# First sums of a graph network: overflow heads loaded alone, gathers two blocks ahead

## The chip, the cores and the metric

One core of a Trainium2 chip runs the whole program in one launch. The metric is the device time in microseconds of that core. The profile is of one execution of the program.

## The reference

The program is a stack of four graph layers over the same graph of 6250 nodes and 200000 edges, each with a residual and a layer norm before it. Two of the layers sum, over the edges of a node, a gated value of the node at the other end. Cut to what the change touches, the first layer computes:

```
gate = silu(edge_attr @ F1W + F1b) @ F2W + F2b
ei = emb[atom_z[src]];  ej = emb[atom_z[dst]]
gate = gate + (ei * (ej @ adapt)).sum(-1, keepdims=True)
msg = gate * h[dst] * (cw * mj)[:, None]
agg = segment_sum(msg, src, N)
tot = clip(segment_sum(mj, src, N), 1e-08)
```

The third layer has the same shape with other weights. Both logits, of the first and third layer, come out of the same pass over the edges (`G` = 32 values of `ei` for each).

## The kernel before

The nodes are padded to 49 blocks (`NB`) of 128 nodes (`P`). An earlier stage sorts the edges into a grid in DRAM: for each node of a block one slot for each of the 49 blocks that an edge can lead to. Each slot is a record of 138 floats (`RW`, 552 bytes), whose column 137 (`HD`) is the head, the number of the node at the other end, or zero where the slot is empty. Edges that find their slot taken go to overflow slots: block `b` has `WS[b]` of them per node, between 4 and 28, 502 over all blocks.

The function `first_sums` runs over the blocks in the order of the list `ORDER`. For one block the 49 slots per node go in four pieces of 14 columns (`PC`; the last one has 7). For these grid pieces the partner's values are picked without a gather: the heads are broadcast (`hr`), compared with the lane number on DVE (`hot_b`, L1187), converted on ACT (L1191) and stored; PE multiplies the one-hot matrices with the table that sits in SBUF (L1007) and ACT copies the result out as `tr` (L1008). The tile `tr` has two buffers. PE also transposes the one-hot matrices (L1198) and ACT gathers them into the tile `dt` (L1199), one row of an adjacency matrix for each node.

The overflow slots are in no block in particular. So their partner's values come by indirect DMA, issued by POOL, one for each slot column (L1085, `tr_o`), from the table in DRAM; the index is worked out on DVE from the head column. One more indirect DMA for each block brings the block's own values `ei` (L1073). The inner function `add` (L1152 to L1178) treats one piece of records, of the grid or of the overflow: bias, product with `ei`, gate, sums on DVE, and copies on ACT that are stored to DRAM. For overflow pieces the addition of the bias is kept in its place in the program by `keep_in_program_order`.

At the end of a block `put_rows` stores the 128 rows of the adjacency matrix (`adj`, one indirect DMA on POOL, L1231). The overflow edges are then written into these rows as single bytes, again by indirect DMAs on POOL, one for each slot column (`put_cells`, L1112). They must wait until the row store has landed. Their addresses (`to`) and values (`many`) are worked out in `overflow` (L1087 to L1107).

What sets the order: each engine executes its instructions in the order of the built program, which a scheduler derives from the source, from the tiles' buffers and from dependencies. Loads of records, of `hr` and the store of the heads are issued by SP. Record tiles (`recs`) form a ring of 8 buffers, shared by grid and overflow pieces; `tr_o` has one buffer of 28 columns, `ei` two. The source's order at the end of a block is:

```
i = put_rows(tc, g.adj, g.nat, b, dt..., "adj")
...
    others, ei, own_cells = overflow(after, hd)
put_cells(*cells_of)
```

In the built program POOL's order in a block is: row store, byte stores of the same block, `ei` of the next block, gathers of the next block.

Of the kernel before, what the change touches and what calls it, by code (L numbers as in the profile page):

```python
# [18 lines left out]
F32 = mybir.dt.float32  # L19
# [5 lines left out]
OP = mybir.AluOpType  # L25
# [4 lines left out]
N, E, H, R, G, NEL, L = 6250, 200000, 48, 40, 32, 119, 4  # L30
P = 128
BIG = 1.0e30
# [3 lines left out]
def rows(t, i):  # L36
    return bass.IndirectOffsetOnAxis(ap=t[:, i : i + 1], axis=0)
# [436 lines left out]
NB = 49  # L474
NQ = NB * P
# [54 lines left out]
def chunks(n, k):  # L530
    return [(i, min(k, n - i)) for i in range(0, n, k)]
# [480 lines left out]
def first_sums(ctx: ExitStack, tc: tile.TileContext, g, keep, dram, table0, tails, h, agg, tot):  # L1012
# [39 lines left out]
    def load(b, spans, src):  # L1052

        out = []
        for s0, n in spans:
            t = sp.tile([P, PC, RW], F32, name="recs", bufs=8)
            if src is over:
                nc.sync.dma_start(t[:, :n], over[b, :, s0 : s0 + n])
            else:
                for k in range(s0, s0 + n, GD):  # L1060
                    v = g.grid[k * NQ : (k + GD) * NQ].rearrange("(r d) f -> r d f", d=GD)
                    nc.sync.dma_start(t[:, k - s0 : k - s0 + GD], v[b * P : (b + 1) * P])
            out.append(t)
        return out

    def overflow(b, hd):


        W = WS[b]
        spans = chunks(W, PC)  # L1070
        recs = load(b, spans, over)
        ei = sp.tile([P, 2 * G + H], F32, name="ei")
        nc.gpsimd.indirect_dma_start(out=ei, out_offset=None, in_=tails, in_offset=rows(g.nat, b))  # L1073
        hv = hd[:, NB : NB + W]
        for (s0, n), t in zip(spans, recs):
            nc.vector.tensor_copy(hv[:, s0 : s0 + n], t[:, :n, HD])
        none = sp.tile([P, OS], F32, name="none", bufs=1)
        nc.vector.tensor_scalar(none[:, :W], hv, 0.0, None, OP.is_equal)
        nc.vector.tensor_scalar(g.bias[:, g.col[b] + NB : g.col[b] + NB + W], none[:, :W], -BIG, None, OP.mult)
        ix = g.idx[:, WO[b] : WO[b + 1]]  # L1080
        nc.vector.tensor_scalar(none[:, :W], none[:, :W], float(NQ), -1.0, OP.mult, OP.add)
        nc.vector.tensor_tensor(ix, hv, none[:, :W], OP.add)
        tr = sp.tile([P, OS, T0], F32, name="tr_o", bufs=1)
        for w in range(W):
            nc.gpsimd.indirect_dma_start(out=tr[:, w], out_offset=None, in_=table0, in_offset=rows(g.idx, WO[b] + w))  # L1085

        mf = sp.tile([P, OS], F32, name="times", bufs=1)  # L1087
        for w, n in chunks(W, 12):
            eq = sp.tile([P, 12, NB + OS], BF, name="same", bufs=1)
            nc.vector.tensor_tensor(eq[:, :n, : NB + W], hd[:, None, : NB + W].to_broadcast([P, n, NB + W]),  # L1090
                                    hv[:, w : w + n, None].to_broadcast([P, n, NB + W]), OP.is_equal)
            nc.vector.tensor_tensor(eq[:, :n, NB : NB + W], eq[:, :n, NB : NB + W],
                                    weights[:, w : w + n, :W], OP.mult)
            nc.vector.reduce_sum(mf[:, w : w + n], eq[:, :n, : NB + W], AX.X)

        to = sp.tile([P, OS], I32, name="to")
        nc.vector.scalar_tensor_tensor(none[:, :W], mf[:, :W], float(AGAIN), none[:, :W], OP.is_ge, OP.add)
        nc.vector.tensor_scalar(none[:, :W], none[:, :W], -1.0, float(1 << 19), OP.not_equal, OP.mult)
        nc.vector.tensor_tensor(none[:, :W], none[:, :W], nat49[:, b : b + 1].to_broadcast([P, W]), OP.add)
        pl = sp.tile([P, OS], I32, name="pl", bufs=1)  # L1100
        nc.vector.tensor_scalar(pl[:, :W], ix, 7, None, OP.logical_shift_right)
        nc.vector.tensor_tensor(to[:, :W], pl[:, :W], none[:, :W], OP.add)
        nc.vector.tensor_scalar(to[:, :W], to[:, :W], 7, None, OP.logical_shift_left)
        nc.vector.tensor_scalar(pl[:, :W], ix, P - 1, None, OP.bitwise_and)
        nc.vector.tensor_tensor(to[:, :W], to[:, :W], pl[:, :W], OP.bitwise_or)
        many = sp.tile([P, OS // 4], I32, name="times_8")
        nc.scalar.activation(many.bitcast(F8)[:, :W], mf[:, :W], AF.Copy, saturate=False)  # L1107
        return [(NB + s0, n, rec, tr[:, s0 : s0 + n]) for (s0, n), rec in zip(spans, recs)], ei, (to, many)

    def put_cells(b, to, many):  # L1110
        for w in range(WS[b]):
# [9 lines left out]
        nc.sync.dma_start(hr[:, : n * P], heads[b : b + 1, d0 * P : (d0 + n) * P].to_broadcast([P, n * P]))  # L1121
        return hr

    def heads_to_rows(b, recs):

        hd = sp.tile([P, NB + OS], F32, name="hd")
        for (s0, n), t in zip(spans, recs):
            nc.vector.tensor_copy(hd[:, s0 : s0 + n], t[:, :n, HD])
        pt = tp.tile([NB, P], F32, name="hd_ps")
        nc.tensor.transpose(pt, hd[:, :NB], ident)  # L1130
        ht = sp.tile([NB, P], BF, name="ht")
        nc.vector.tensor_scalar(ht, pt, firsts, None, OP.subtract)
        nc.sync.dma_start(heads[b].rearrange("(d p) -> d p", p=P), ht)
        bs = g.bias[:, g.col[b] : g.col[b] + NB]
        nc.vector.tensor_scalar(bs, hd[:, :NB], 1.0, -1.0, OP.min, OP.add)
        nc.vector.tensor_scalar(bs, bs, BIG, None, OP.mult)
        return [heads_of(b, *span) for span in spans[:2]], hd

    recs = load(ORDER[0], spans, g.grid)
    hrs, hd = heads_to_rows(ORDER[0], recs)  # L1140
    others, ei, own_cells = overflow(ORDER[0], hd)
    for pos, b in enumerate(ORDER):
        after = ORDER[pos + 1] if pos + 1 < NB else None
        T = NB + WS[b]
        nc.scalar.copy(h[:, pos], ei[:, 2 * G :])
        lgt = sp.tile([P, NB + OS], F32, name="lgt")
        bs = g.bias[:, g.col[b] : g.col[b] + T]
# [4 lines left out]
        def add(t0, n, rec, tr):  # L1152
            rec = rec[:, :n]
            at = sp.tile([P, PC, R], F32, name="at", bufs=2)
            nc.scalar.copy(at[:, :n], rec[:, :, :R])
            nc.scalar.dma_start(g.attr[b, :, t0 : t0 + n], at[:, :n])
            g2 = sp.tile([P, PC, H], F32, name="g2", bufs=2)
            nc.scalar.copy(g2[:, :n], rec[:, :, R + H : CW])
            nc.scalar.dma_start(g.gate[b, :, t0 : t0 + n], g2[:, :n])
            i = nc.vector.tensor_add(bs[:, t0 : t0 + n], bs[:, t0 : t0 + n], tr[:, :n, T0 - 1])  # L1160
            if t0 >= NB:
                tc.keep_in_program_order(i)

            pr = sp.tile([P, PC, 2 * G], F32, name="pr", bufs=1)
            nc.vector.tensor_mul(pr[:, :n], tr[:, :n, H : H + 2 * G], ei[:, None, : 2 * G].to_broadcast([P, n, 2 * G]))
            lg = sp.tile([P, PC, 2], F32, name="lg")
            nc.vector.reduce_sum(lg[:, :n], pr[:, :n].rearrange("p t (k g) -> p t k g", k=2), AX.X)
            nc.vector.tensor_mul(lg[:, :n, 0], lg[:, :n, 0], rec[:, :, CW])
            nc.vector.tensor_mul(lgt[:, t0 : t0 + n], lg[:, :n, 1], rec[:, :, CW])

            ga = pr[:, :, :H]
            nc.vector.tensor_add(ga[:, :n], rec[:, :, R : R + H], lg[:, :n, 0:1].to_broadcast([P, n, H]))
            if not done:
                nc.vector.memset(acc, 0.0)
            nc.vector.tensor_mul(ga[:, :n], ga[:, :n], tr[:, :n, :H])
            nc.vector.tensor_add(acc[:, :n], acc[:, :n], ga[:, :n])
            nc.vector.reduce_sum(ac[:, len(done)], tr[:, :n, T0 - 2], AX.X)
            done.append(t0)  # L1178


        dt = sp.tile([P, NB, P], F8, name="dt", bufs=1)
# [11 lines left out]
        for i, (s0, n) in enumerate(spans):  # L1193
# [6 lines left out]
            tr = sp.tile([P, PC, T0], F32, name="tr")  # L1200
            pick_rows(nc, pp, lambda d: hot[d // HC][:, d % HC * P : (d % HC + 1) * P], parts, T0, tr, s0, n, 4)
            add(s0, n, recs[i], tr)
            if i == 1 and after is not None:
                ahead = load(after, spans, g.grid)
        if after is not None:
            hrs, hd = heads_to_rows(after, ahead)
        for piece in others:
            add(*piece)
        i = put_rows(tc, g.adj, g.nat, b, dt.rearrange("p d q -> p (d q)").bitcast(I32), "adj")
        tc.declare_no_dep(i.ins, group="cells", reason="the cells before are in rows of other nodes")  # L1210
        cells_of = b, *own_cells
        nc.scalar.dma_start(g.logit[b, :, :T], lgt[:, :T])
        add_up(nc, acc, PC, agg[:, pos])
        nc.vector.reduce_sum(tot[:, pos : pos + 1], ac[:, : len(done)].rearrange("p i o -> p o i"), AX.X)
        if after is not None:
            recs = ahead
            others, ei, own_cells = overflow(after, hd)
        put_cells(*cells_of)


def add_up(nc, t, n, to):
# [623 lines left out]
```

## Time and profile before

| | |
|---|---|
| median of 9 runs | 13152.42 us |
| lowest and highest run | 13143.89 and 13208.33 us |
| profiled execution | 13151.98 us, span 13150.0 us |
| busy over the span | DVE 7871.8 us (60%), POOL 7144.7 us (54%), PE 5622.2 us (43%), ACT 3877.6 us (29%) |
| granted TensorE clock, mean | 0.658 |
| first sums, about 4530 to 6980 us | DVE busy 1430.7, POOL 1174.9, ACT 1157.5, PE 926.5 us (4530 to 6980) |
| DMA queues in the stage, share of 16 engines | q1 (SP) 35.8%, q10 (ACT) 18.8%, q0 (POOL) 12.3% |
| row stores of the stage | 49, the first at 4570.8 us, the last at 6960.3 us |

A group of the profile reads: line, engine, operation, names of output and inputs, count, then busy time and the mean of one in ns, then the idle time of the engine just before these instructions and what ended it. A wait reads: engine, tile and line that waited, then what released it, then the total in us, the number of waits and the longest. A line of the timeline gives start and duration, and in brackets the idle time before the instruction and its releaser. "issue" is time in which the engine waited for nothing that the profile shows.

### The profile page before, as it was taken

Reading aid. Unit: us, or ns where it says so; the run is one execution under the profiler, and the core shown is the slowest. Engines: PE = TensorE matmul, PEld = TensorE weight load, DVE = VectorE, ACT = ScalarE, POOL = GpSimd, SP = SyncE. Lnnn points to the kernel's source line nnn. Section 1 sums busy time; section 2 is a strip of 40 time slices with the busy share of each in tenths; the row PEclk is TensorE's granted clock in tenths of the full one; section 3 lists DMA queues with packets and bytes.
Section 4 is the critical chain, followed back from the end, with each engine's and each line's share of the span. In section 5 each row is a group of like instructions: output and inputs, shape, how many; then the busy total and the mean of one; then the engine's idle time right before and its main releaser. Section 6 shows DMA issues by size and latency. Waiting matters only on the chain. (4 is left out here: it accounts for less than half of the span.)

```text
span 13150.0 us, 180013 instructions
## 1 busy us (share of the span) xinstructions
PE 5622.2 (43%) x67611; PEld 4825.2 (37%) x67611; DVE 7871.8 (60%) x16470; ACT 3877.6 (29%) x9495; POOL 7144.7 (54%) x5713
## 2 busy tenths in 40 slices
PE   1154444444444333333333543444354344393225
PEld 1133333333333233333332443444344344393225
DVE  7644444444444365555555988788698688714443
ACT  0033333333333244444442322322232222211111
POOL 0344444444444344544443887688588588705881
PEclk9965556656556566666655766676676676696557
DMA  8733312222222366766662443444344344474445
GB/s 292 266 101 101 98 52 60 56 54 57 56 56 53 100 222 212 221 219 213 225 200 83 136 124 105 118 127 125 98 129 124 96 129 128 122 221 118 131 124 148
DMA packets 970522, 1742.53 MB, mean 133 GB/s; under 512 B 478058, under 2 KB 686158, under 8 KB 911909
## 3 DMA queue, kind: packets, MB, share of 16 engines
q1 hardware_dynamic: 645378, 1038.72, 25.5%
q0 software_dynamic: 188320, 315.39, 10.7%
q10 hardware_dynamic: 135936, 376.80, 7.4%
q8 instruction: 531, 8.70, 0.3%
q14 instruction: 357, 2.92, 0.1%
HBM read 1176.43 MB, written 561.07 MB: 132 GB/s over the span
## 5 line engine op out<-in xcount | busy, mean ns | idle before, releaser
L1258 POOL DMA_INDIRECT over<-table_k,idx_g x2008 | 3017.4, 1503 | 847.7 <-issue 578.1
L1007 PEld LDWEIGHTS <-hot_t 128*128 128x128 fp8e4 x36015 | 1933.5, 114 | 2588.5 <-issue 2569.7
L975 POOL DMA_INDIRECT grid<-rec,sloti x1666 | 1709.6, 1026 | 2122.2 <-DVE rec L946 1075.8
L1007 PE MATMUL pick_ps<-k_parts,hot_t 128*128 128x96 bf16 x28812 | 1739.7, 233 | 1774.0 <-ACT kh L1008 1137.2
L1008 ACT COPY kh<-pick_ps 128x480 f32<-128x480 f32 (+1 forms) x1960 | 983.8, 567 | 1676.8 <-DVE sm L1227 478.0
L1258 POOL DMA_INDIRECT over<-table_g,idx_g x502 | 721.1, 1436 | 607.4 <-DMA lg<-logit 441.9
L971 PEld LDWEIGHTS pg<-w,hid 97*128 97x128 f32 x3332 | 594.0, 262 | 959.1 <-ACT hid L968 822.8
L972 DVE TENSOR_TENSOR rec<-pg,cut 128x384 f32<-128x384 f32 (+1 forms) x441 | 235.4, 534 | 1085.4 <-remote 863.8
L971 PE MATMUL pg<-w,hid 97*128 97x96 f32 x3332 | 683.2, 362 | 388.5 <-ACT hid L968 329.1
L1007 PE MATMUL pick_ps<-table_b,hot_b 128*128 128x114 bf16 x7203 | 658.9, 268 | 406.1 <-issue 310.7
L1112 POOL DMA_INDIRECT adj<-times,to x502 | 562.4, 1120 | 466.9 <-DMA adj<-dt,nat 254.8
L916 ACT ACTIVATE junk<-dup_ps,less 128x128 bf16<-128x128 f32 x1666 | 594.3, 367 | 634.4 <-PE dup_ps L913 283.7
L901 DVE TENSOR_TENSOR pick<-look_ps,sb 128x441 f32<-128x441 f32 x588 | 346.5, 590 | 719.7 <-remote 409.5
L899 PE MATMUL look_ps<-look,low 128*128 128x147 bf16 x1666 | 454.7, 279 | 748.6 <-DVE look L894 688.3
L1007 PEld LDWEIGHTS <-hot_b 128*128 128x128 bf16 x7203 | 588.0, 130 | 469.4 <-issue 469.0
L968 ACT ACTIVATE hid<-ph,w1b 96x512 f32<-96x512 f32 (+1 forms) x441 | 291.6, 661 | 1572.7 <-remote 850.1
L1198 PE MATMUL dt_ps<-f_identb,hot_b 128*128 128x128 bf16 x2401 | 291.5, 277 | 909.3 <-DVE hot_b L1187 473.1
L966 PE MATMUL ph<-at,w1s 120*96 120x512 bf16 (+1 forms) x1323 | 521.5, 509 | 292.0 <-issue 195.9
L1225 DVE TENSOR_TENSOR kh<-kh 128x1152 f32<-128x1152 f32 (+4 forms) x980 | 609.9, 623 | 0.0
L1007 PE MATMUL pick_ps<-g_parts,hot_t 128*128 128x48 bf16 x7203 | 289.9, 205 | 703.5 <-ACT xe L1008 376.6
L1085 POOL DMA_INDIRECT tr_o<-table,idx_g x502 | 491.8, 980 | 170.1 <-issue 148.4
L1326 DVE TENSOR_TENSOR kh<-kh,sc 128x2352 f32<-128x2352 f32 x196 | 510.0, 2602 | 107.6 <-ACT sc L1323 52.3
(419 smaller groups left out, 13903.0 us busy)
## 6 DMA issues: line engine op xcount, KB each, us to landing
hot_t<-hot SPq DMA_DIRECT2D x245, 784.0 KB
grid<-zero ACTq DMA_DIRECT2D x150, 1127.0 KB
recs<-grid SPq DMA_DIRECT2D x348, 483.0 KB
am<-adj SPq DMA_DIRECT2D x147, 784.0 KB
hr<-heads_g SPq DMA_DIRECT2D x147, 448.0 KB
low<-lows SPq DMA_DIRECT2D x49, 1088.0 KB
gate_g<-g ACTq DMA_DIRECT2D x156, 336.0 KB
attr_g<-at ACTq DMA_DIRECT2D x156, 280.0 KB
```

The lines of the kernel that those rows point to most:

```text
L899: nc.tensor.matmul(ps[:, t], slt[:, t0 + t], lk[:, t0 + t], start=True, stop=True)
L916: nc.scalar.activation(junk, ps[:, t], AF.Sign, bias=less13[:, way : way + 1], accum_out=dup[:, t0 + t : t0 + t + 1])
L966: nc.tensor.matmul(ph[:, : n * P], w1s[:, k], at[:, : n * P], start=(k == 0), stop=(k == 2))
L971: nc.tensor.matmul(pg[:, k], ht[:, k * P : (k + 1) * P], w2, start=True, stop=True)
L975: i = nc.gpsimd.indirect_dma_start(out=g.grid, out_offset=rows(sloti, t), in_=rec[:, t, :], in_offset=None, bounds_check=SLOTS - 1, oob_is ...
L1007: nc.tensor.matmul(ps[:, d], hot(db0 + d0 + d), parts[:, db0 + d0 + d, k], start=(k == 0), stop=(k == 2))
L1008: nc.scalar.copy(dst[:, d0 : d0 + m], ps[:, :m])
L1085: nc.gpsimd.indirect_dma_start(out=tr[:, w], out_offset=None, in_=table0, in_offset=rows(g.idx, WO[b] + w))
L1112: i = nc.gpsimd.indirect_dma_start(out=cells, out_offset=rows(to, w), in_=many.bitcast(U8)[:, w : w + 1], in_offset=None, bounds_check=NQ ...
L1225: nc.vector.tensor_add(t[:, :k], t[:, :k], t[:, n - k : n])
L1258: self.tc.nc.gpsimd.indirect_dma_start(out=t[:, w], out_offset=None, in_=self.table, in_offset=rows(self.g.idx, WO[b] + w0 + w))
L1326: nc.vector.tensor_mul(v, v, sc[:, :NB, None].to_broadcast([P, NB, H]))
```

## The change

The head column of the overflow slots is loaded alone into a tile `hv` (function `seek`), three blocks ahead, with 4 buffers. `index` works out the bias and the index from it two blocks ahead. `gather` issues `ei` (now 3 buffers) and the gathers of the overflow pieces two blocks ahead; `tr_o` is now a tile of 14 columns with 3 buffers. In the source these gathers stand behind the row store, and the byte stores stand behind the last of them under `tc.issue_after`. The rest of `overflow`, the addresses and values of the byte stores, is `cells_to`. The overflow pieces come first in the block instead of last, the addition of their bias is no longer kept in program order, the overflow records are loaded after the third grid piece of the block before, and the record ring has 7 buffers for 8. The numbers of gathers, byte stores and row stores stay as they are.

```diff
-            t = sp.tile([P, PC, RW], F32, name="recs", bufs=8)
+            t = sp.tile([P, PC, RW], F32, name="recs", bufs=7)
...
-    def overflow(b, hd):
...
+    def seek(pos):
+
+        if pos >= NB:
+            return None
+        hv = sp.tile([P, OS, 1], F32, name="hv", bufs=4)
+        nc.sync.dma_start(hv[:, : WS[ORDER[pos]]], over[ORDER[pos], :, : WS[ORDER[pos]], HD : HD + 1])
+        return hv.rearrange("p w o -> p (w o)")
+
+    def index(pos, hv):
+
+        b = ORDER[pos]
         W = WS[b]
...
+        none = sp.tile([P, OS], F32, name="none", bufs=4)
+        nc.vector.tensor_scalar(none[:, :W], hv[:, :W], 0.0, None, OP.is_equal)
...
+        nc.vector.tensor_tensor(g.idx[:, WO[b] : WO[b + 1]], hv[:, :W], none[:, :W], OP.add)
+        return hv, none
+
+    def gather(pos):
+
+        b = ORDER[pos]
+        ei = sp.tile([P, 2 * G + H], F32, name="ei", bufs=3)
         nc.gpsimd.indirect_dma_start(out=ei, out_offset=None, in_=tails, in_offset=rows(g.nat, b))
...
+        for s0, n in chunks(WS[b], PC):
+            tr = sp.tile([P, PC, T0], F32, name="tr_o", bufs=3)
+            for w in range(n):
+                last = nc.gpsimd.indirect_dma_start(out=tr[:, w], out_offset=None, in_=table0,
+                                                    in_offset=rows(g.idx, WO[b] + s0 + w))
+            out.append((NB + s0, n, tr))
+        begun.append(last.ins)
+        return ei, out
+
+    def cells_to(b, hd, hv, none):
...
+    begun = []
+    sought = [seek(pos) for pos in range(3)]
+    found = [index(pos, sought.pop(0)) for pos in range(2)]
+    gathered = [gather(pos) for pos in range(2)]
...
             i = nc.vector.tensor_add(bs[:, t0 : t0 + n], bs[:, t0 : t0 + n], tr[:, :n, T0 - 1])
-            if t0 >= NB:
-                tc.keep_in_program_order(i)
...
+        for (t0, n, tr), rec in zip(others, recs_over):
+            add(t0, n, rec, tr)
...
+            if i == 0 and pos + 2 < NB:
+                found.append(index(pos + 2, sought.pop(0)))
+                sought.append(seek(pos + 3))
             if i == 1 and after is not None:
                 ahead = load(after, spans, g.grid)
+            if i == 2 and after is not None:
+                recs_over = load(after, chunks(WS[after], PC), over)
...
-        for piece in others:
-            add(*piece)
         i = put_rows(tc, g.adj, g.nat, b, dt.rearrange("p d q -> p (d q)").bitcast(I32), "adj")
         tc.declare_no_dep(i.ins, group="cells", reason="the cells before are in rows of other nodes")
-        cells_of = b, *own_cells
+        if pos + 2 < NB:
+            gathered.append(gather(pos + 2))
+
+        with tc.issue_after(begun[-1]):
+            put_cells(b, *own_cells)
...
-            others, ei, own_cells = overflow(after, hd)
-        put_cells(*cells_of)
+            own_cells = cells_to(after, hd, *found.pop(0))
```

More of the change, by code (lines that the diff above doesn't have):

```diff
@@ L1064, in load @@
         return out
-    def overflow(b, hd):
-        W = WS[b]
[L1070 to L1079, printed above, removed]
-        ix = g.idx[:, WO[b] : WO[b + 1]]
[L1081 to L1085, printed above, removed]
+    def seek(pos):
[4 more added lines that the diff above has]
+        return hv.rearrange("p w o -> p (w o)")
@@ new lines, in index @@
+    def index(pos, hv):
+        b = ORDER[pos]
+        W = WS[b]
+        none = sp.tile([P, OS], F32, name="none", bufs=4)
+        nc.vector.tensor_scalar(none[:, :W], hv[:, :W], 0.0, None, OP.is_equal)
+        nc.vector.tensor_scalar(g.bias[:, g.col[b] + NB : g.col[b] + NB + W], none[:, :W], -BIG, None, OP.mult)
+        nc.vector.tensor_scalar(none[:, :W], none[:, :W], float(NQ), -1.0, OP.mult, OP.add)
+        nc.vector.tensor_tensor(g.idx[:, WO[b] : WO[b + 1]], hv[:, :W], none[:, :W], OP.add)
+        return hv, none
@@ new lines, in gather @@
+    def gather(pos):
+        b = ORDER[pos]
+        ei = sp.tile([P, 2 * G + H], F32, name="ei", bufs=3)
+        nc.gpsimd.indirect_dma_start(out=ei, out_offset=None, in_=tails, in_offset=rows(g.nat, b))
+        out = []
+        for s0, n in chunks(WS[b], PC):
[6 more added lines that the diff above has]
+        return ei, out
@@ L1087, in overflow @@
+    def cells_to(b, hd, hv, none):
+        W = WS[b]
+        ix = g.idx[:, WO[b] : WO[b + 1]]
         mf = sp.tile([P, OS], F32, name="times", bufs=1)
@@ L1107, in overflow @@
         nc.scalar.activation(many.bitcast(F8)[:, :W], mf[:, :W], AF.Copy, saturate=False)
-        return [(NB + s0, n, rec, tr[:, s0 : s0 + n]) for (s0, n), rec in zip(spans, recs)], ei, (to, many)
+        return to, many
     def put_cells(b, to, many):
@@ L1122, in heads_of, with heads_to_rows @@
         return hr
-    def heads_to_rows(b, recs):
+    def heads_to_rows(b, recs, hv):
         hd = sp.tile([P, NB + OS], F32, name="hd")
@@ L1128, in heads_to_rows @@
             nc.vector.tensor_copy(hd[:, s0 : s0 + n], t[:, :n, HD])
+        nc.vector.tensor_copy(hd[:, NB : NB + WS[b]], hv[:, : WS[b]])
         pt = tp.tile([NB, P], F32, name="hd_ps")
@@ L1137, in heads_to_rows @@
         return [heads_of(b, *span) for span in spans[:2]], hd
+    begun = []
+    sought = [seek(pos) for pos in range(3)]
+    found = [index(pos, sought.pop(0)) for pos in range(2)]
+    gathered = [gather(pos) for pos in range(2)]
     recs = load(ORDER[0], spans, g.grid)
-    hrs, hd = heads_to_rows(ORDER[0], recs)
-    others, ei, own_cells = overflow(ORDER[0], hd)
+    recs_over = load(ORDER[0], chunks(WS[ORDER[0]], PC), over)
+    hrs, hd = heads_to_rows(ORDER[0], recs, found[0][0])
+    own_cells = cells_to(ORDER[0], hd, *found.pop(0))
     for pos, b in enumerate(ORDER):
@@ L1144, in first_sums @@
         T = NB + WS[b]
+        ei, others = gathered.pop(0)
         nc.scalar.copy(h[:, pos], ei[:, 2 * G :])
@@ L1202, in first_sums @@
             add(s0, n, recs[i], tr)
+            if i == 0 and pos + 2 < NB:
+                found.append(index(pos + 2, sought.pop(0)))
+                sought.append(seek(pos + 3))
             if i == 1 and after is not None:
                 ahead = load(after, spans, g.grid)
+            if i == 2 and after is not None:
+                recs_over = load(after, chunks(WS[after], PC), over)
         if after is not None:
-            hrs, hd = heads_to_rows(after, ahead)
-        for piece in others:
-            add(*piece)
+            hrs, hd = heads_to_rows(after, ahead, found[0][0])
         i = put_rows(tc, g.adj, g.nat, b, dt.rearrange("p d q -> p (d q)").bitcast(I32), "adj")
         tc.declare_no_dep(i.ins, group="cells", reason="the cells before are in rows of other nodes")
-        cells_of = b, *own_cells
+        if pos + 2 < NB:
+            gathered.append(gather(pos + 2))
+        with tc.issue_after(begun[-1]):
+            put_cells(b, *own_cells)
         nc.scalar.dma_start(g.logit[b, :, :T], lgt[:, :T])
```

## The prediction

> **What bounds the kernel now.** I read four views: the granted clock, the windows, the groups of the stage between 4530 and 6980 us, and in there the waits and a timeline of one block. The windows say that no resource is full in the stage that the diff touches. The columns are us, busy us of PE, PEld, DVE, ACT and POOL, then the granted clock, the DMA share and GB/s:
>
> ```profile
> 5500.00:6000.00 500.00, 193.49 (x2010) 168.92 (x2010) 294.54 (x805) 239.42 (x378) 242.79 (x227) 0.62 0.67 217
> ```
>
> DVE is busy 59%, POOL 49%, the DMA engines 67%. So the stage is held by a chain of waits, and POOL's four groups show which (busy, mean ns, idle before):
>
> ```profile
> L1112 POOL DMA_INDIRECT adj<-times,to x502 | 562.4, 1120 | 466.9 <-DMA adj<-dt,nat 254.8 <-issue 146.9 <-DVE bias L1160 19.0
> L1085 POOL DMA_INDIRECT tr_o<-table,idx_g x502 | 491.8, 980 | 170.1 <-issue 148.4 <-DVE pl L1101 11.0 <-DVE pr L1175 3.7
> L1231 POOL DMA_INDIRECT adj<-dt,nat x49 | 69.2, 1411 | 620.3 <-ACT dt L1199 607.1 <-ACT h_rows L1145 10.2 <-issue 3.0
> L1073 POOL DMA_INDIRECT ei<-tails,nat x47 | 51.6, 1097 | 22.0 <-issue 12.8 <-DVE none L1099 5.9 <-DVE pr L1165 2.7
> ```
>
> Busy and idle of the rows add to 1029.3 + 661.9 + 689.5 + 73.6 = 2454.3 us, the whole stage, or 50 us for each of 49 blocks. Two of the three big waits face each other:
>
> ```profile
> POOL adj L1231 <- ACT dt L1199: 607.1, 45, 31.2
> DVE ac L1177 <- DMA tr_o<-table,idx_g: 538.8, 45, 21.6
> POOL adj L1112 <- DMA adj<-dt,nat: 254.8, 37, 9.6
> DVE bias L1160 <- DMA tr_o<-table,idx_g: 39.9, 5, 18.2
> ```
>
> POOL waits for ACT before the row store, while DVE waits for POOL's gathers. One block in order of time shows the ring (the last gather, DVE's stall, two of the four grid pieces, the row store, the last grid piece, the first byte store):
>
> ```profile
> 5497.30 0.95 POOL L1085 DMA_INDIRECT tr_o<-table,idx_g  x1 [0.30 <-issue]
> 5501.03 0.17 DVE L1177 TENSOR_REDUCE ac<-tr_o 128x1 f32<-128x9 f32 x1 [13.77 <-DMA tr_o<-table,idx_g]
> 5501.21 1.08 DVE L1165 TENSOR_TENSOR pr<-tr,ei 128x896 f32<-128x896 f32 x1
> 5506.34 1.09 DVE L1165 TENSOR_TENSOR pr<-tr,ei 128x896 f32<-128x896 f32 x1
> 5511.12 1.55 POOL L1231 DMA_INDIRECT adj<-dt,nat  x1 [12.87 <-ACT dt L1199]
> 5518.01 1.34 POOL L1112 DMA_INDIRECT adj<-times,to  x1 [5.34 <-DMA adj<-dt,nat]
> 5519.45 0.62 DVE L1165 TENSOR_TENSOR pr<-tr,ei 128x448 f32<-128x448 f32 x1
> ```
>
> Gathers land, DVE runs on, tiles `tr` come free, ACT can make the last `dt`, the row store goes, lands, the byte stores go, the gathers behind them go, and DVE waits for those. Over the 49 blocks the means are 8.1 us from row store to first byte store, 13.7 for the byte stores, 14.6 for `ei` and gathers, 13.4 from last gather to the next row store: 49.8.
>
> **What the change does to this ring.** The order of instructions in the built program decides, not the source. Three things stand in it. Gathers do run further ahead: positions 0 to 3 are gathered before the first row store (31 gathers, 4 before), then position k+4 or k+3 behind row store k. But the byte stores of block k still stand directly behind row store k, ahead of those gathers. And with the pinned order of the overflow bias addition gone, DVE executes that addition for the gathers behind byte stores k inside block k+1, before or in its first grid piece, three blocks before the value is used. For 43 of the 50 gathered pieces after the start it stands there. So DVE, which executes in order, still waits in every block for gathers issued straight behind the byte stores. Distance in the source is three blocks, distance on DVE is one, as before. The 578.7 us of DVE waiting (538.8 + 39.9) change their line, not their place.
>
> **The sum,** against the profiled execution: 13151.98 us, 2 us over its span and 0.4 below the median of the runs, so no correction.
>
> 1. *`ei` leaves the gather stretch.* It is issued between row store and byte stores, while POOL waits anyway. All of row L1073 goes: 51.6 + 22.0 = −73.6.
>
> 2. *The byte stores wait for `ei`.* `ei` has 3 buffers, so the load for block k+3 overwrites that of block k and waits on POOL for DVE's last read of it, the multiplication of the fourth grid piece. Queued behind it on POOL: the byte stores, then the gathers that DVE waits for. In the block above this read ends at 5519.45 + 0.62 = 5520.1; one issue (1.10 + 0.30) makes 5521.4, against 5518.0. Over all blocks the read ends 9.0 us after the row store; with 1.3 for the issue 10.3 against 8.1, thus 2.2 × 48 = +105. Ends: 0 if the reads come sooner, +120 if only the late blocks count (2.5 each). I take 105.
>
> 3. *27 gathers more before the loop:* 27 × (0.98 + 0.30) = 34 us. Their cover is POOL's idle time up to the first row store at 4570.8, some 30 us. The last three blocks in turn have none left. Gain 34 if all of it shortens the ring, nothing if DVE sets those last blocks: I take −18.
>
> 4. *49 loads of the head column* on SP's queue, each of W × 128 (mean 1311) separate 4-byte elements. The nearest row is a load of 6144 four-byte elements in the first stage; the next issue on the queue stood 14.05 us behind it, 2.3 ns an element:
>
> ```profile
> 3.64 14.05 SPq L1464 DMA_DIRECT2D mu<-in_node_vec_dram  x1
> ```
>
> That makes 3.0 us a block, 147 in all. As a share of the engines it is less: between 3 and 20 us the queue's 6365 packets took 22.6% of 16 engines, 0.6 ns each, which makes 0.8 us a block, 39 in all. The loads are wanted three blocks later, so they hide themselves; what they push is the broadcast `hr` and the records on the same queue, for which DVE waits already (62.7 us at L1187, 98.3 at L1128). Ends 0 and +147, taken +40, the second price, as SP spends 1237.9 of the stage's 2450 us waiting for a free buffer of records.
>
> The Trainium skill ("DMA: Bandwidth & Descriptors", Rules for kernel authors) says that a strided last dimension lowers to one descriptor per element, which speaks against this load. Its section Measured gives about 10.5 ns a packet at the floor: by that the loads would take an estimated 14 us a block and the sum would be some 630 us higher; the row above is over four times cheaper.
>
> 5. *One buffer of records less* (7 for 8). SP waits for a free one already, far ahead of use; the reader's own wait is the 98.3 us at L1128. Ends 0 and +50 (half of that row), taken +10.
>
> 6. *Gathers beside a busy DVE.* They mostly run now while DVE stands still and take 0.98 us; byte stores beside a working DVE take 1.12, and single gathers in such stretches 1.69:
>
> ```profile
> 5371.63 1.69 POOL L1085 DMA_INDIRECT tr_o<-table,idx_g  x1 [0.30 <-issue]
> ```
>
> So 502 × 0.14 = +70 at most. Against it, DVE's stall stands up to one piece's multiplications later in the block (about 1.5 us of 43 blocks: −65 at most). I book the two against each other at 0 and keep both ends.
>
> The small operations (index and bias from the column, one copy more and up to two less per block, 0.17 us each on DVE) and the wait of 50.4 us at L1076 for overflow records, which ends sooner, are covered by DVE's stall; uncovered they are worth 10 us.
>
> Sum: −73.6 + 105 − 18 + 40 + 10 = +63, thus 13215 us. All ends together span −173 to +313; taken as independent (half-widths 60, 17, 73, 25, 68) they make about ±120.
>
> **Rivals.** *Faster, the ring opens:* DVE does not wait in the next block, for instance because most gathers land before their bias addition comes up. The 578.7 us then go, and next late is POOL itself (2454 − 607 = 1847 us) or the DMA engines (0.67 × 50 = 33 us a block). All of it gives 12575, half 12865. For it: nothing is full. Against it: the place of the addition in DVE's order. It decides where the gathers end 12 us or more earlier than now relative to DVE's first grid piece (538.8 us over 45 waits). Chance 0.09.
>
> *Faster, a little:* `ei`'s last read comes before the row store has landed, item 2 falls to 0, and items 1 and 3 remain: 13152 − 92 + 50 = 13110. For it: the blocks in which the read is early. Chance 0.11.
>
> *No change:* item 2 at a third, or the later stall, cancels the rest. Between 13126 and 13178: chance 0.13.
>
> *Slower by the column loads:* item 4 at 3.0 us on the path, since `hr` stands behind it: 13215 + 107 = 13322. For it the 14.05 us row, against it the three blocks' time. Chance 0.17.
>
> *The forecast,* slower by the wait for `ei`: 0.50.
>
> **How the numbers follow.** Runs of before lie within 13144 to 13169 but for one, so less than 0.2%, 26 us, can't be told from no change. Slower 0.50 + 0.17 = 0.67, same 0.13, faster 0.20. The range takes the small gain at its far end, 13060, and the column loads with the ring's price, 13340. Outside stand the open ring (0.09) and about 0.09 of both tails.
>
> **What would show it.** Right: POOL's byte stores begin about 10 us after the row store; the wait before `ei` names DVE's multiplication by `ei` at the fourth piece, some 350 us in all; DVE's wait for `tr_o` stays near 540 us, now at the bias addition; POOL's wait for ACT's `dt` stays near 600. For single steps: the column loads' time on SP's queue near 1 us (item 4), waits for `hr` and records not above 62.7 and 98.3 us (items 4, 5), gathers still near 0.98 us (item 6). Wrong: DVE's wait for `tr_o` under 300 us and a block of 45 us or less (the ring opened), or waits for `hr` grown by over 100 us (the column loads). The Trainium skill ("GPSIMD Engine Reference", Specifications) says that GpSimd shares its SBUF interfaces with VectorE; the 1.69 us gather would fit that, but no run here separates it.

## The result and the profile after

The changed kernel takes 13227.02 us (median of 10 runs, 13206.6 to 13269.65) against 13154.81 us of the kernel before (31 runs, the nine of the table above among them). The medians are 72 us apart, and the ratio is 1.006, 95% interval 1.0047 to 1.0073. The forecast was 13215 us, with 0.67 on slower.

The profiled execution after took 13247.56 us. Of its 95.8 us more span, 29.6 lie ahead of the stage: the last store of the grid is issued at 4508.5 us against 4478.9. The change does not touch that part, so these 29.6 us are not counted below.

The window of the stage reads as before, no resource is full (us, busy us of PE, PEld, DVE, ACT, POOL, then granted clock, DMA share and GB/s):

```profile
5500.00:6000.00 500.00, 195.74 (x1885) 170.83 (x1886) 272.55 (x767) 224.71 (x353) 246.69 (x227) 0.61 0.67 211
```

POOL's four groups over the stage (4500 to 7080 us; busy, mean ns, idle before and its releasers):

```profile
L1130 POOL DMA_INDIRECT adj<-times,to x502 | 548.2, 1092 | 201.4 <-issue 169.3 <-DMA adj<-dt,nat 16.9 <-DVE lg L1190 7.6
L1094 POOL DMA_INDIRECT tr_o<-table,idx_g x502 | 494.0, 984 | 176.3 <-issue 148.9 <-DVE pr L1198 18.2 <-DVE to L1123 5.1
L1263 POOL DMA_INDIRECT adj<-dt,nat x49 | 96.5, 1970 | 571.1 <-ACT dt L1225 571.1
L1089 POOL DMA_INDIRECT ei<-tails,nat x49 | 54.1, 1105 | 390.4 <-DVE pl L1122 257.3 <-DVE none L1117 55.2 <-DVE pr L1188 48.1
```

They add to 749.6 + 670.3 + 667.6 + 444.5 = 2532 us, 78 more than the 2454 before. The row to look at is the last: `ei` was 73.6 us in all and is now 444.5, nearly all of it waiting. What the byte stores lost (1029.3 to 749.6, because their wait for the landing row store fell from 254.8 to 16.9 us) is less than what `ei` took. A wait was not removed; another one was put ahead of it in the same place.

The waits show that the two big ones kept their size:

```profile
POOL adj L1263 <- ACT dt L1225: 559.5, 48, 23.5
DVE bias L1185 <- DMA tr_o<-table,idx_g: 543.4, 45, 20.6
POOL ei L1089 <- DVE pl L1122: 257.3, 29, 11.7
DVE hot_b L1213 <- DMA hr<-heads_g: 185.1, 109, 5.1
DVE hd L1146 <- DMA recs<-grid: 144.0, 89, 5.2
POOL adj L1130 <- DMA adj<-dt,nat: 16.9, 2, 8.6
```

DVE waited 578.7 us for gathers before (two lines) and waits 543.4 now, at the bias addition. Its wait for `hr`, 185.1 us, was this before:

```profile
DVE hot_b L1187 <- DMA hr<-heads_g: 62.7, 47, 5.3
```

And one block in order of time:

```profile
5607.16 0.17 DVE L1185 TENSOR_TENSOR bias<-bias,tr_o 128x8 f32<-128x8 f32 x1 [10.94 <-DMA tr_o<-table,idx_g]
5615.60 2.51 POOL L1263 DMA_INDIRECT adj<-dt,nat  x1 [12.32 <-ACT dt L1225]
5625.44 0.62 DVE L1188 TENSOR_TENSOR pr<-tr,ei 128x448 f32<-128x448 f32 x1
5625.98 0.17 DVE L1122 TENSOR_SCALAR pl<-idx_g 128x12 int32<-128x12 int32 x1
5626.34 1.25 POOL L1089 DMA_INDIRECT ei<-tails,nat  x1 [8.22 <-DVE pl L1122]
5627.89 1.08 POOL L1130 DMA_INDIRECT adj<-times,to  x1 [0.30 <-issue]
```

The load of `ei` starts 0.3 us after the multiplication by `ei` of the fourth piece has ended (5625.44 + 0.62 = 5626.06). The profile names L1122 as the releaser. That is the neighbour on DVE that ended nearest before (5626.15). The trace shows that it was the multiplication: POOL's first instruction for this load, one that no view lists, starts at 5626.11, 0.03 us after L1188 has raised its count and before L1122 has ended, and the same distance stands ahead of 42 of the 46 loads of `ei` inside the loop. Where the named releaser makes no sense as a dependency, look at the instructions around it.

From the trace, means over the 48 blocks from one row store to the next (us):

| | before | after |
|---|---|---|
| row store to first byte store | 8.08 | 12.13 |
| byte stores | 14.78 | 14.17 |
| `ei` (before) and gathers behind them | 14.47 | 13.15 |
| last gather to next row store | 12.45 | 11.41 |
| block | 49.78 | 50.85 |
| last grid store to first row store, once | 91.9 | 113.4 |

The forecast counted to the start of the last issue of each list, the table counts to its end, so its 13.7, 14.6 and 13.4 us are the 14.78, 14.47 and 12.45 of this table; the means after are over all 48, though the last three blocks have no gathers left.

48 × 1.07 = 51 us in the blocks and 21.5 us at the start make 73; the program behind the stage is 6.7 us shorter. These are single executions, so that 73 meets the 72 of the medians so closely is chance. The 51 us are a balance: the first 45 blocks are 1.7 us longer each (50.04 to 51.73), the last three together 25 us shorter.

### The profile page after: what moved, and what is told of

Read it like the earlier page. It is cut to its first block, busy times and chain, and to the rows that moved or that the text cites. A ratio compares the mean times of both kernels' runs of the same rounds, so it can differ in the third digit from the quotient of the medians.

```text
span 13245.8 us, 180258 instructions
## 1 busy us (share of the span) xinstructions
PE 5660.5 (43%) x67611; PEld 4870.0 (37%) x67611; DVE 7850.0 (59%) x16465; ACT 3874.3 (29%) x9495; POOL 7165.1 (54%) x5713
## 3 DMA queue, kind: packets, MB, share of 16 engines
q0 software_dynamic: 188320, 315.39, 10.6%
## 5 line engine op out<-in xcount | busy, mean ns | idle before, releaser
L1007 PE MATMUL pick_ps<-table_b,hot_b 128*128 128x114 bf16 x7203 | 685.7, 276 | 454.9 <-issue 293.0
L1007 PEld LDWEIGHTS <-hot_b 128*128 128x128 bf16 x7203 | 618.1, 135 | 509.8 <-issue 509.5
L1224 PEld LDWEIGHTS <-hot_b 128*128 128x128 bf16 x2401 | 235.8, 133 | 982.0 <-issue 569.2
```

The costliest lines, as they stand in the source:

```text
L1007: nc.tensor.matmul(ps[:, d], hot(db0 + d0 + d), parts[:, db0 + d0 + d, k], start=(k == 0), stop=(k == 2))
L1224: nc.tensor.transpose(pd[:, k], hot[d // HC][:, d % HC * P : (d % HC + 1) * P], identb)
```

## The experiments

The experiments ran on three chips, each beside the kernel before, which took 13138.26 us (e1 to e4), 11619.98 us (e5 to e8) and 13033.54 us (e9 to e12). So ratios to the kernel before are what may be compared, and the us in the expectations for e5 to e8 fit the first chip only. From chip to chip even the ratio of one kernel can move (e8 and e12 below). The changed kernel was not run beside e1 to e8; where they are set against it, its 1.006 is that of the result above, and e9 has it at 1.0073 on the third chip.

**e1_pin: the bias addition kept in order again.**

```diff
             i = nc.vector.tensor_add(bs[:, t0 : t0 + n], bs[:, t0 : t0 + n], tr[:, :n, T0 - 1])
+            if t0 >= NB:
+                tc.keep_in_program_order(i)
```

> The changed kernel with the bias addition of the overflow pieces kept in program order again, as before the change. Theory (the ring stays closed because DVE executes that addition in the very next block): DVE's first read of a block's gathers now stands one to two blocks behind their issue, so its wait for tr_o falls from 543 us to under 100 and the block from 50.9 us to between 40 and 45: 12850 to 12960 us. Rival (the look-ahead was never worth anything, because the wait would only move to the DMA engines or to SP's loads, which are 70% busy): block 49 to 51 us, 13170 to 13230 us, with DVE's waits for hr and records grown by what the wait for tr_o loses.

Measured: 13052.44 us, ratio 0.9948 (0.9929 to 0.9966), faster than both kernels. The order of POOL and SP is the same as in the changed kernel, and on ACT and PE two pairs change places; what differs is DVE's order. The groups of the stage for the overflow pieces' bias addition, first of the changed kernel, then of e1, and the waits of POOL and DVE in e1:

```profile
L1185 DVE TENSOR_TENSOR bias<-bias,tr_o 128x14 f32<-128x14 f32 (+13 forms) x54 | 9.4, 174 | 553.0 <-DMA tr_o<-table,idx_g 543.4 <-issue 9.6
L1185 DVE TENSOR_TENSOR bias<-bias,tr_o 128x14 f32<-128x14 f32 (+13 forms) x54 | 9.1, 169 | 0.0
```

```profile
POOL adj L1265 <- ACT dt L1227: 394.4, 43, 17.6
DVE hot_b L1215 <- DMA hr<-heads_g: 217.8, 118, 5.5
POOL ei L1089 <- DVE pl L1122: 208.7, 27, 11.7
DVE bias L1185 <- ACT tr L1008: 203.3, 33, 33.9
```

The idle time before the addition goes from 553.0 us to 0.0: the two lines of source decided whether DVE waits for the newest gathers. But the block falls only from 50.85 to 46.92 us, not to 40 to 45. The row store still waits 394 us for ACT, and DVE now waits for `hr` and for ACT's copies. So the mechanism of the theory is shown and its price was too high: 543 us of waiting were worth about 1.1% of the time, some 147 us (ratios 1.006 and 0.9948; their intervals leave 30 us either way).

**e2_ei_free: `ei` without its wait.**

```diff
-        ei = sp.tile([P, 2 * G + H], F32, name="ei", bufs=3)
+        ei = sp.tile([P, 2 * G + H], F32, name="ei", bufs=4)
...
+            with tc.issue_after(row):   # row: the row store of two blocks before
                 nc.gpsimd.indirect_dma_start(out=ei, out_offset=None, in_=tails, in_offset=rows(g.nat, b))
```

> The changed kernel with ei one buffer more and its load tied behind the row store of two blocks before its use, so that it overwrites a tile whose last read is a block back; nothing else is touched, the addition is still hoisted. Theory (item 2 of the sum: the byte stores wait for the last read of ei): the time from row store to first byte store falls from 12.1 us to the 8.1 of before, and each block is up to 4 us shorter, 13030 to 13110 us. Rival (that wait lies beside another that ends as late): under 30 us from the 13227 of the changed kernel.

Measured: 13161.09 us, ratio 1.0015 (1.0002 to 1.0029). POOL's byte stores and `ei` in the stage:

```profile
L1134 POOL DMA_INDIRECT adj<-times,to x502 | 550.6, 1097 | 485.7 <-DMA adj<-dt,nat 300.9 <-issue 166.3 <-DVE lg L1194 8.1
L1093 POOL DMA_INDIRECT ei<-tails,nat x47 | 51.5, 1095 | 14.3 <-issue 14.3
```

The wait before `ei` is gone (390.4 to 14.3 us), and the wait for the landing row store is back (16.9 to 300.9, more than the 254.8 before the change). The first byte store stands 10.37 us after the row store, not 8.1, and the block is 49.69 us. So taking the wait for `ei` away shortens that stretch by 1.8 us and the block by 1.2 us; by the ratios (1.006 and 1.0015) it is worth 59 us, between 34 and 84 by their intervals, most of the loss. And both sides of the expectation missed: the gain is twice the rival's 30 us and half or less of the theory's. The remaining 2.3 us are the row store's own: its issue takes 1.98 us (1.41 before), the first of its 128 packets starts 5.6 us after the issue has begun (3.8 before), and the last one ends after 9.0 us (7.0 before; means over the 49 row stores, from the packets in the traces). Why it is later was not tried.

**e3_order and e4_pin_order: gathers really ahead of the byte stores,** the second with the pin of e1 as well.

```diff
-            gathered.append(gather(pos + 2))
+            with tc.issue_after(i.ins):
+                gathered.append(gather(pos + 2))
```

> The changed kernel with the whole gather of block k+2, ei included, tied behind row store k, so that POOL's order is row store, ei, gathers, byte stores; the addition is still free to be hoisted. Theory: the byte stores leave the ring, which is now row store, gathers (13 us), DVE, ACT, row store; DVE still waits for gathers in the next block but these are issued 24 us earlier: block 41 to 45 us, 12870 to 13000 us. Rival (any order that keeps both lists of indirect DMAs in a block keeps the time): above 13150 us.

> Both: addition pinned and gathers ahead of the byte stores. Theory: either edit alone opens the ring, the next limit is reached by either, so the two together are within 40 us of the better one. Rival (two independent costs): the gains add, and it is over 150 us faster than the better one.

Measured: 12933.49 us, ratio 0.9846 (0.9827 to 0.9866), and 12922.88 us, ratio 0.9842 (0.9826 to 0.9859). The edit holds the gathers back: in the changed kernel the scheduler issues them as early as buffers allow, three to four blocks ahead, so the instruction behind which the byte stores were to be tied is long past, and the byte stores follow the row store at once. With the edit POOL's order is row store, `ei`, gathers of block k+2, byte stores. Of e3, DVE's bias addition, POOL's byte stores and its row store in the stage:

```profile
L1185 DVE TENSOR_TENSOR bias<-bias,tr_o 128x14 f32<-128x14 f32 (+13 forms) x54 | 9.5, 176 | 69.8 <-DMA tr_o<-table,idx_g 37.0 <-DMA adj<-times,to 18.0 <-issue 14.0
L1130 POOL DMA_INDIRECT adj<-times,to x502 | 541.2, 1078 | 171.9 <-issue 161.9 <-DVE lg L1190 8.2 <-DMA tr_o<-table,idx_g 0.6
L1264 POOL DMA_INDIRECT adj<-dt,nat x49 | 65.4, 1334 | 692.8 <-ACT dt L1225 692.8
```

The byte stores no longer wait for the row store, since the row store lands under the gathers, and DVE's wait falls to 37.0 us although the addition is still hoisted. The block is 45.06 us. That lies within the 12870 to 13000 us of its theory. Adding the pin changes nothing that can be told (45.45 us), as the theory of e4 said: both edits open the same ring. Behind it stands POOL's wait of 693 us for ACT's `dt`; what holds up `dt` there was not taken apart.

**e5_column_twice and e10_column_twice: the column load issued twice;** e9_after is the changed kernel on the chip of e10.

```diff
-        nc.sync.dma_start(hv[:, : WS[ORDER[pos]]], ...)
+        for _ in range(2):
+            nc.sync.dma_start(hv[:, : WS[ORDER[pos]]], ...)
```

> The changed kernel with the load of the head column issued twice into the same tile; the second load brings the same data. Theory of the forecast's item 4 (0.8 us a block on the path, 39 us in all): 13245 to 13285 us. Rival (3.0 us a block at the price of the first stage's load, 147 us): 13340 to 13390. Third (hidden, since it is wanted three blocks later): within 15 us of 13227.

> The changed kernel itself, to stand on one chip with the three others of this call. Its ratio to the kernel before was 1.006: expected 1.004 to 1.008 again, whatever the chip's own level.

> The column load issued twice, now beside the changed kernel on one chip. Theory (0.8 us a block on the path): 30 to 50 us above e9_after. Rival (3.0 us a block): 110 to 160 above. Third (hidden): within 15 us of it, which its ratio of 1.0056 in the run before lets expect.

Measured: e5 ratio 1.0056 (1.0039 to 1.0073); on the third chip the changed kernel 13127.29 us, ratio 1.0073 (1.0055 to 1.0091), and the doubled load 13114.76 us, ratio 1.0073 (1.0052 to 1.0094). The queue of the loads in e9 and e10 (packets, MB, share of 16 engines):

```profile
q1 hardware_dynamic: 710418, 1038.98, 25.7%
q1 hardware_dynamic: 775458, 1039.24, 26.1%
```

65040 packets more, and no time: the second load is hidden.

**e6_ring7: the kernel before with 7 record tiles.**

```diff
-            t = sp.tile([P, PC, RW], F32, name="recs", bufs=8)
+            t = sp.tile([P, PC, RW], F32, name="recs", bufs=7)
```

> The kernel before with the ring of record tiles at 7 in place of 8, nothing else. Theory of the forecast's item 5: 10 us, between 0 and 50, so 13140 to 13190 us. Rival (the ring is what SP's 1237.9 us of waiting stand for, and one tile less shifts every load): over 100 us slower.

Measured: 11567.65 us, ratio 0.9956 (0.9939 to 0.9973), on the second chip: faster, which neither side expected. Another ring size also lets the scheduler place other instructions elsewhere; what of it makes the gain was not taken apart, and on the other chips it was not run.

**e7_pin_ei_free: pin and free `ei` together,** the edits of e1 and e2.

> The changed kernel with the bias addition pinned and ei tied behind the row store with one buffer more. The pin alone gave 13052, ei alone 13161, the changed kernel 13227. Theory (with the pin POOL's own chain is the ring: row store 10.6 us to first byte store, byte stores, gathers; of these the wait for ei, 8.96 us from row store to ei against 2.3, is what ei's buffer takes away, down to the landing of the row store): 2 us a block less than the pin alone, 12930 to 12990. Rival (DVE's own waits for hr and ACT's copies hold the block at 47 us): within 30 us of 13052.

Measured: 11289.62 us, ratio 0.9724 (0.9705 to 0.9744), 41.18 us a block, on the second chip. POOL's row store in the stage:

```profile
L1269 POOL DMA_INDIRECT adj<-dt,nat x49 | 60.0, 1225 | 110.2 <-ACT dt L1231 99.2 <-issue 9.2 <-ACT h_rows L1174 0.6
```

Here POOL hardly waits for ACT: its own chain (9.1 us to the first byte store, most of it the landing of the row store, 14.8 byte stores, 15.2 gathers) is 39 of the 41 us. That is the limit that the forecast's first rival named. How much of the step from e1 is the edit and how much the chip can't be told, because e1 was not run there.

**e8_order_column_act, e11_order, e12_order_column_act: the column load on ACT's queue,** with the order of e3.

```diff
-        nc.sync.dma_start(hv[:, : WS[ORDER[pos]]], ...)
+        nc.scalar.dma_start(hv[:, : WS[ORDER[pos]]], ...)
```

> Gathers of block k+2 with ei behind row store k, ahead of the byte stores (12933 us), and the load of the head column issued on ACT's queue in place of SP's. Theory (the column load stands ahead of hr on SP's queue, which is why DVE's wait for hr grew from 63 to 188 us): that wait falls under 100 us and the time by 50 to 100, 12830 to 12890 us. Rival (the wait for hr has another cause, such as two buffers of hr and a block that is shorter): within 25 us of 12933, and the wait stays over 150 us.

> Gathers of block k+2 ahead of the byte stores, the column load on SP. Theory (byte stores out of the ring): 1.5% to 3% faster than before on any chip, as the 0.9846 of e3_order.

> The same with the column load on ACT's queue. Theory (the column load holds up hr on SP's queue): 50 to 100 us below e11_order, with the wait for hr lower by as much. Rival (hr is late for another cause): within 25 us of e11_order, and the 0.9679 of e8_order_column_act came from its chip.

Measured: e8 11247.8 us, ratio 0.9679 (0.9663 to 0.9695) on the second chip. Side by side on the third: e11 12801.25 us, ratio 0.9825 (0.9806 to 0.9844), and e12 12827.33 us, ratio 0.9851 (0.9828 to 0.9874). Moving the load off SP's queue brings nothing; DVE's wait for `hr` goes from 191.4 us (e11) to 151.6 (e12), and the time does not follow:

```profile
DVE hot_b L1213 <- DMA hr<-heads_g: 191.4, 100, 7.1
DVE hot_b L1213 <- DMA hr<-heads_g: 151.6, 83, 4.0
```

So the column is some 40 us of that wait at most, and not what sets the time; the step from 0.9851 to 0.9679, with one and the same kernel, belongs to the chip.

The order of e3 is the version to keep: it beats both kernels on two chips, 1.5% to 1.75% below the kernel before, with one edit.

## Why the prediction was right, and where its steps were off

The sign and the cause hold: distance in the source is not distance on the engine. DVE's wait for gathers stayed (543.4 us where 540 was said), POOL's for ACT stayed (559.5, 600 said), the block did not shrink, and the load of `ei` put DVE's last read ahead of the byte stores (361 us of waits for DVE, 350 said). e1 shows that it was the unpinned addition, e2 that the wait for `ei` made most of the loss.

The total of +63 against +72 is closer than its terms. Item by item:

1. *`ei` out of the gather stretch,* and 3. *27 gathers ahead of the loop.* Booked −73.6 and −18. The gather stretch got 1.32 us a block shorter, 63 us. Half of that, 32 us, are the last three blocks, whose gathers item 3 moved; the 45 others got 0.71 us shorter, 32 us in place of the 73.6 of item 1, with new waits for DVE (18.2 and 5.1 us) in them. The start got 21.5 us longer. Item 3 counted POOL's idle time as a cover for these gathers, and not that DVE, in its order, reads all four gathered positions before its first grid piece (up to the first row store it waits 29.6 us for `tr_o`, 5.8 before). e1, where it does not, starts after 104.4 us, and e3, with 9 gathers ahead of the loop, after 95.2, not 113.4. Together −42 instead of −92.

2. *The byte stores wait for `ei`.* Sized 2.2 us a block, measured 4.05. This is the term that was most wrong. It was read off the trace of before, where the last read of `ei` ends 9.0 us after the row store, and taken to stay there. In the changed kernel it ends 10.6 us after the row store, and from there to the first byte store it is 1.5 us where 1.3 was said (means over 48 blocks, from the traces). Between row store and that read DVE now has the next block's comparison `hot_b` (1.0 us a block, 0.07 before), its wait for `hr` (1.73 us, 0.12 before) and more of the sums `times` (0.67 us, 0.13 before); before, waits for overflow records and `tr_o` stood there (1.64 us). e2 wins back only 1.8 of the 4.05 us, because the landing of the row store, 2 us later than before, is next; the sum had no term for that either.

4. *Column loads.* Booked +40; doubling them cost nothing (1.0073 and 1.0073). The forecast's own test for this rival, a wait for `hr` grown by over 100 us, came true (62.7 to 185.1 us) and was a bad test: with the load doubled (190.1 us against 169.8) and with it on another queue the time stayed. What made DVE's wait for `hr` grow stays open (with 7 record tiles and no column load, in e6 on the second chip, it is 112.9 us; the kernel before was not profiled there); it is not the column load that sets the time. The price itself was near: the 64904 more 4-byte packets of the stage took 9.07 ns each on their engine, 36.8 us of all 16 engines' time where 39 was said. They took it beside the path. The rule of the Trainium skill ("DMA: Bandwidth & Descriptors", Rules for kernel authors), one descriptor per element, agrees with the count: 65040 packets more than before on the queue, 502 × 128 = 64256 of them elements. The price per packet of that page's section Measured would have made it the largest term, and the run shows it hidden.

5. *Ring of 7.* Booked +10, measured in the kernel before as a gain of 0.44% on the one chip where it ran. The sign was wrong there; in the changed kernel it was not tried.

6. *Gathers beside a busy DVE, and the later stall.* Gathers take 0.984 us in the changed kernel, as in the one before (0.980), where DVE still mostly stands still beside them (busy in 15% of their time, 12% before). In e1 and e3, where it works in 40% and 55% of it, they take 1.08, two thirds of the way to the bound of 0.14 us more; in e7, on the second chip, 1.17 at 68%, past it. From last gather to row store 1.04 us a block were gained, 50 us, within the −65 to 0 of the later stall. The zero booked for the two missed these 50.

From the booked +63 to the trace: item 2 adds 89 (1.85 × 48), items 1 and 3 add 50; items 4 and 5, which were not found, take off 50, item 6 takes off 50, and the byte stores, a little quicker without a term of their own (0.61 us a block), 29. That makes 73. The terms cancel better than they were sized; that the sum came within 10 us is luck.

*The open ring,* the rival at 0.09, did not happen in the changed kernel, but its condition was named rightly: where the addition stands in DVE's order. Its price was not. Half of the 578.7 us was to give 12865, all of it 12575. e1 takes the whole wait away and gains about 147 us against the changed kernel, where by its waits ACT's `dt` and copies, `hr` and `ei` are next late and not POOL's own issues; which of them sets the time was not tried on that chip. e3 gains 281 (ratios 1.006 and 0.9846).

## What to carry to other kernels

A look-ahead is as long as the shortest distance between an issue and the first reader in any engine's order, and a scheduler that may move the reader forward undoes it: read the built order of the reading engine, and pin the reader or hold the load back. A load that is moved ahead brings the wait for its own buffer with it, to the front of everything queued behind it on its engine. When a wait goes, price the gain by what is late next, not by the size of the wait: here 543 us of waiting were worth about 147.

## What was not expected of the hardware

The chips here differ more than the kernels do. The kernel before took 13138, 11620 and 13034 us on three chips, and the same edit (column load on ACT's queue, with the order of e3) gave 0.9679 on the second and 0.9851 on the third. On the second chip the stage starts near 3220 us, on the others at about 4440 to 4510, so most of its lead lies before the first sums; in e8 the DMA engines there moved 268 GB/s at a share of 0.82 (4000 to 4500 us) where the same kernel (e12) on the third shows 231 GB/s and 0.72 (5000 to 5500 us). Why was not settled.

The row store's issue on POOL is not a constant: 1.41 us before, 1.97 in the changed kernel, 1.29 in e1 and 1.33 in e3, for the same 128 rows. Nor is the time from the start of the issue to its first packet: 3.8, 5.6, 4.8 and 4.9 us. None of the runs shows why.
